# Graph attention, two layers on 32 graphs: keys and values of two tiles by seven half-depth products

## The chip, the core and the metric

The kernel runs on one core of one Trainium2 chip. A core has a matrix engine (TensorE, PE in the profile, with its weight loads as PEld), three engines for elementwise work (VectorE or DVE, ScalarE or ACT, GpSimd or POOL), and a queue engine (SyncE, SP) that issues transfers. Matmuls write to PSUM, eight banks of 2 KB in each of 128 partitions; everything else lives in SBUF. The metric is the time of one execution on the device in microseconds. Five runs of the kernel before gave a median of 2818.61 us (2816.21 to 2819.26).

## The reference

`x` is 32 graphs of 512 nodes with 512 features, `adj` a 512 x 512 matrix of zeros and ones with about 4 ones in a row, one for all graphs. All numbers are float32.

```python
# layer 0
h = relu(layernorm(x))
q, k, v = h @ Wq + bq, h @ Wk + bk, h @ Wv + bv        # 8 heads of 64
scores = q @ k.T / 8 + (1 - adj) * -1e9                # per head
x = x + softmax(scores) @ v @ Wo + bo
# layer 1
h = relu(layernorm(x))
g = h @ W
s1, s2 = g @ a1, g @ a2
e = leaky_relu(s1[:, None] + s2[None, :], 0.2) * adj
x = x + elu(softmax(e) @ g + beta * g)
```

## The kernel before

**Tiles.** A graph is a batch `b` of T = 4 tiles of P = 128 nodes; a tile's features are C = 4 blocks of 128. Since a row of `adj` has few ones, the kernel never forms 512 x 512 scores. It sorts the nodes once (`edges`), so that each group of 32 nodes of a tile has at most 128 edges, and then works on lists of 128 edges: four lists a tile, one for each of the groups `g`. For every batch it

- *stage_a(b)*: fetches x by an indirect transfer (`fetch`, POOL), normalises it (`norm`: DVE, then a power on POOL, line 724, then DVE), applies relu (ACT), turns it by four transposes on TensorE into `hT`, and multiplies `hT` with wk, wv and wq (`dense`, four chained 128x512 products each, recorded at line 41). DVE adds the bias to k and q (line 788), ACT copies v (line 782). SP stores k, v and q to tables in DRAM (`put`).
- *stage_b(b)*: for each tile gathers rows of the table by edge (`kv`, line 826, k and v of layer 0 together with h of layer 1 of the graph two batches earlier) and rows of q (`qe`, line 842), four of each. `layer0` multiplies q by k (line 869), sums by head (line 872), exponentiates and weighs v (ACT, lines 878 and 883: 32 small activations a tile). Then `edge_sums` (line 857) adds up the edges of each node by a product with a 0/1 matrix `OH`: for each group of 32 nodes one product with 32 columns of weights, four groups beside each other in the array. The sums are divided (lines 902, 906), turned, multiplied with wo, added to x (line 920), normalised; the result `hx` is stored for layer 1.
- `layer1` does the same for the graph two batches earlier: weights of edges `wv` (line 994), `edge_sums`, the denominator (lines 1007 to 1009), own share (line 1015), transposes, an addition of column sums (line 1028), the product with W, elu (lines 1037 to 1043), and an indirect store (line 742).

Two row sums at the end of each batch, over v (line 800) and over hx (line 947), use the same array shape as the edge sums, with 512 columns.

**Order.** Nothing is ordered by hand directly. Each step is an `op` with an engine, an estimated duration and a key (its due time, in units where a tile is S = 20). `Plan.order` simulates the engines and takes, of what can start now on an engine, the lowest key; TensorE may wait 0.3 us for a lower key and adds 1.0 to the key of an op of another array shape (`form`). The order so found is the fixed order of every engine's instructions; at run time each waits for what it needs by semaphores. Stage_a of a batch is due six tiles ahead of its stage_b.

**Rings.** Buffers come from `rings`, each with so many buffers; an op that takes one can't be planned before one is free. `reserve` takes the buffer of a result when the product before it starts. PSUM: ring D has 4 banks for all dense products and transposes, ring X has 2 buffers of two banks each for the edge sums. "Free order" rings (D, X) may be taken out of order.

**Batch 0** differs: x comes in plain order, and k, v and q are stored by indirect transfers on POOL, since the sort is not known when it starts.

Of the kernel before, what the change touches and what calls it, by code (L numbers as in the profile page):

```python
# [19 lines left out]
P = 128  # L20
HD = 64
# [191 lines left out]
def kernel(  # L213
# [49 lines left out]
    def ring(n, shape, name):  # L263
# [4 lines left out]
        "hT": ring(2, [P, C, P], "hT"),  # L268
        "oT": ring(2, [P, C, P], "oT"),
        "gT": ring(2, [P, C, P], "gT"),  # L270
        "q": ring(4, [P, D], "q"),
# [3 lines left out]
        "qe": ring(3, [P, 2, D], "qe"),  # L275
        "o": ring(2, [P, D], "o"),
        "x1": ring(4 * LAG + 1, [P, D], "x1"),
        "hx": ring(4, [P, HW_], "hx"),
        "g": ring(2, [P, D], "g"),
        "y": ring(2, [P, D], "y"),  # L280
# [8 lines left out]
        "dn": ring(6, [P, 3], "dn"),  # L289
        "s1": ring(2, [P, T], "s1"),  # L290
        "s1t": ring(1, [T, P], "s1t"),
# [8 lines left out]
        "D": [psum.tile([P, D], F32, name=f"pd{i}", tag=f"pd{i}") for i in range(4)],  # L300
        "X": [psum.tile([P, 2, D], F32, name=f"px{i}", tag=f"px{i}") for i in range(2)],
    }
    plan = Plan(rings, ("D", "X"))
    buf, op = plan.buf, plan.op

    ones = wtile([P, P], "ones")
# [9 lines left out]
    dmax = wtile([P, T, 2], "dmax")  # L316
# [7 lines left out]
        "rmax", "dmax", "bad", "cap", "flag", "perm", "posi",  # L324
    )}

    def setup():
# [3 lines left out]
        nc.gpsimd.memset(ones, 1.0)  # L331
        nc.gpsimd.memset(mhalf, -0.5)
        zero = rings["kv"][-1]
        nc.vector.memset(zero[:, 0, :HW_], 0.0)
# [9 lines left out]
    def constants():  # L344
# [7 lines left out]
        zero = rings["kv"][-1]  # L352
        for tag, n in (("tk", D), ("tkv", D), ("qtab", D), ("th", HW_), ("tab", ROW)):
            for tab in rings[tag]:
                for c0, c1 in ((0, D), (HO, ROW)) if tag == "tab" else ((0, n),):
                    m = 1 if tag == "qtab" else DUMMY
                    load(lambda tab=tab, c0=c0, c1=c1, m=m: nc.sync.dma_start(
                        tab[N:, c0:c1], zero[:m, 0, : c1 - c0]))
# [11 lines left out]
    def edges():  # L370
# [5 lines left out]
        jp, nbb, pr, col = buf("q", "jp"), buf("q", "nb"), buf("q", "pr"), buf("g", "col")  # L376
        sd, val, sc, Eb = buf("kv", "scr2"), buf("kv", "val"), buf("kv", "scr"), buf("kv", "E")

        def flat(b):
            return b.ap.rearrange("p a b -> p (a b)")  # L380
# [42 lines left out]
        op("PE", 1.0, key, lambda: product(nc, pk.ap, ones, flat(sd)[:, :N]), r=[sd], w=[pk])  # L423
# [29 lines left out]
        op("PE", 1.0, key, lambda: product(nc, pp.ap, ones, flat(sd)[:, :N]), r=[sd], w=[pp])  # L453
# [124 lines left out]
        en = buf("kv", "en")  # L578
# [62 lines left out]

    def value_row():
        bvc, bvr = buf("g", "bvc"), buf("oT", "bvr")
# [16 lines left out]
    def dot_rows():  # L660
        wa = buf("s1", "wa"), buf("s1", "wa")
        for g in range(2):
            ar, scr, row = buf("y", "ar"), buf("o", "scr"), buf("row", "wrow")
# [80 lines left out]

    def put(b, dst, t, src, key, part, w):
# [8 lines left out]
    def stage_a(b):  # L754
# [3 lines left out]
        for t in range(T):  # L758
            key = base(T * b + t - AHEAD) if b else 2.0 + 0.4 * S * t
            xb = buf("x", f"x{b}_{t}")  # L760
            if b:
                op("POOL", 1.3, key - 2.0 * S, lambda xb=xb, t=t: fetch(xb.ap, b, t), r=[C_["perm"]], w=[xb], dma=P * D * 4)
            else:
                op("SP", 0.1, -90.0 + 0.01 * t, lambda xb=xb, t=t: nc.sync.dma_start(xb.ap, x[0, ts(t, P), :]), w=[xb], dma=P * D * 4)
            norm(key - 1.3 * S, xb, mv, t, f"a{b}_{t}")
            op("ACT", 0.8, key - 0.9 * S, lambda xb=xb, t=t: relu(xb.ap, xb.ap, mv.ap, t), r=[(mv, t)], w=[xb])
            pt, hT = buf("D", "pt"), buf("hT", f"hT{b}_{t}")
            o = op("PE", 0.45, key - 0.51 * S, lambda pt=pt, xb=xb: turned(pt.ap, xb.ap), r=[xb], w=[pt])
            plan.reserve(o, hT)

            op("ACT", 0.6, key - 0.51 * S, lambda pt=pt, hT=hT: nc.scalar.copy(  # L771
                hT.ap.rearrange("p c q -> p (c q)"), pt.ap), r=[pt], w=[hT])
            q, k, v = buf("q", f"q{b}_{t}"), buf("k", f"k{b}_{t}"), buf("v", f"v{b}_{t}")
            vs.append(v)
            for i, (w, n, dst) in enumerate(((wk, "wk", k), (wv, "wv", v), (wq, "wq", q))):
                p = buf("D", "p" + n)
                kk = key + (0.12, 0.30, 0.56)[i] * S
                o = op("PE", 3.43, kk, lambda p=p, hT=hT, w=w: dense(p.ap, hT.ap, w),
                       r=[hT, C_[n]], w=[p])
                plan.reserve(o, dst)  # L780
                if n == "wv":
                    op("ACT", 0.62, kk, lambda p=p, v=v: nc.scalar.copy(  # L782
                        v.ap[:, :, 0:HD], p.ap.rearrange("p (h f) -> p h f", f=HD)), r=[p], w=[v])
                    tab, cols = place(b, VO, H * VW)
                    put(b, cols, t, lambda v=v: v.ap.rearrange("p h f -> p (h f)"), kk, v, [(tab, ("v", t))])
                else:
                    row = {"wq": bq_r, "wk": bk_r}[n]
                    op("DVE", 0.7, kk, lambda p=p, dst=dst, row=row: nc.vector.tensor_tensor(  # L788
# [27 lines left out]
    def stage_b(b):  # L816
# [14 lines left out]
        for t in range(T):  # L831
# [16 lines left out]
            if old is not None:  # L848
                layer1(b - LAG, t, kb, slots)
# [445 lines left out]
```

## Time and profile before

| | |
|---|---|
| median of five runs | 2818.61 us |
| profiled execution, its own time | 2821.35 us |
| its span, first to last instruction | 2819.6 us |
| mean granted TensorE clock | 0.991 |
| dense products (line 41: wo, wk, w, wv, wq), records | 1032 + 4 x 1024 |
| edge sums (line 857), records | 2 x 2048 |
| transposes (line 712), records | 640 + 512 + 512 |
| DMA, mean rate | 283 GB/s, 796.83 MB |
| windows 300 to 800, 800 to 1300, 1300 to 1800 us | TensorE busy 500.00 of 500 in each; DMA share 0.84, 0.84, 0.86 |
| last 119 us | TensorE busy 91.5, DMA share 0.59 |

A float32 product is two records of matmul, so a dense product of four blocks is eight records; the durations given for single matmuls overlap, and times between starts are what counts. Rows of groups give line, engine, operation, output and inputs by the program's names, shape and count; then busy time and the mean of one in ns; then the idle time of the engine just before them and what ended it. A row of the waits gives engine, what was about to run, what it waited for, the time in all, how often, and the longest.

### The profile page before, as it was taken

How to read it: one execution, taken by the hardware profiler on the slowest of the kernel's cores; microseconds unless marked ns; L12 is line 12 of the kernel's file. 1: busy time of each engine (PE TensorE's matmuls, PEld its weight loads, DVE VectorE, ACT ScalarE, POOL GpSimd, SP SyncE). 2: the span in 40 equal slices, each digit the busy share in tenths (PEclk: the TensorE clock that was granted, in tenths of full speed). 3: DMA queues.
4: the chain of work that ended last, by engine and by line, in shares of the span. 5: the costliest groups of instructions: out<-in, count | busy, mean ns of one | idle time of the engine just before them, and what ended most of it. 6: DMA issues, size and time to landing. Idle time of an engine off the chain costs nothing. (4 is left out here: it accounts for less than half of the span.)

```text
span 2819.6 us, 41845 instructions
## 1 busy us (share of the span) xinstructions
PE 2759.1 (98%) x11506; PEld 1290.9 (46%) x11506; DVE 1894.5 (67%) x4556; ACT 1940.5 (69%) x6241; POOL 1890.0 (67%) x1730
## 2 busy tenths in 40 slices
PE   7999999999999999999999999999999999999977
PEld 3444444444444444444444444444444444444433
DVE  6466667666666666666666666666766666666674
ACT  1476777676677677677677677677677777677774
POOL 2787666676666676666676766666766666666665
PEclk9999999999999999999999999999999999999989
DMA  5889888888888888888888888888888888888875
GB/s 166 233 292 328 301 297 288 287 291 284 299 295 287 287 289 289 298 293 293 284 287 293 293 292 298 279 288 297 290 291 300 276 287 302 284 294 295 274 252 149
DMA packets 242344, 796.83 MB, mean 283 GB/s; under 512 B 35587, under 2 KB 35715, under 8 KB 242102
## 3 DMA queue, kind: packets, MB, share of 16 engines
q0 software_dynamic: 157056, 643.94, 68.1%
q1 hardware_dynamic: 85046, 150.15, 14.8%
q8 instruction: 93, 1.52, 0.2%
q14 instruction: 149, 1.22, 0.1%
HBM read 624.70 MB, written 169.26 MB: 282 GB/s over the span
## 5 line engine op out<-in xcount | busy, mean ns | idle before, releaser
L883 ACT ACTIVATE kv<-kv 128x64 f32<-128x64 f32 x4096 | 1006.2, 335 | 6.2
L826 POOL DMA_INDIRECT kv<-tab,idx x480 | 517.3, 1078 | 331.8 <-PE px L857 219.0
L842 POOL DMA_INDIRECT qe<-qtab,qidx x512 | 555.1, 1084 | 177.5 <-issue 123.4
L869 DVE TENSOR_TENSOR qe<-qe,kv 128x1024 f32<-128x1024 f32 x256 | 313.6, 1225 | 282.1 <-DMA kv<-tab,idx 171.0
L41 PE MATMUL pd<-wo,oT 128*128 128x512 f32 x1032 | 475.2, 604 | 8.9 <-DVE k L788 4.5
L41 PE MATMUL pd<-wk,hT 128*128 128x512 f32 x1024 | 474.0, 606 | 0.3 <-ACT hT L771 0.3
L41 PE MATMUL pd<-w,gT 128*128 128x512 f32 x1024 | 463.1, 595 | 2.6 <-ACT gT L1028 2.6
L41 PE MATMUL pd<-wv,hT 128*128 128x512 f32 x1024 | 462.8, 595 | 0.7 <-ACT hT L771 0.7
L41 PE MATMUL pd<-wq,hT 128*128 128x512 f32 x1024 | 460.9, 593 | 0.8 <-ACT v L782 0.8
L737 POOL DMA_INDIRECT x<-in_x_dram,perm x252 | 340.8, 1352 | 78.5 <-issue 49.6
L724 POOL TENSOR_TENSOR mv<-mv,mhalf 128x1 f32<-128x1 f32 x256 | 225.0, 881 | 202.1 <-DVE mv L721 161.7
L872 DVE TENSOR_REDUCE s<-qe 128x16 f32<-128x1024 f32 x256 | 310.7, 1214 | 2.1
L41 PEld LDWEIGHTS pd<-wo,oT 128*128 128x128 f32 x1032 | 196.9, 194 | 247.7 <-issue 232.8
L41 PEld LDWEIGHTS pd<-wv,hT 128*128 128x128 f32 x1024 | 195.4, 191 | 246.2 <-issue 238.5
L41 PEld LDWEIGHTS pd<-w,gT 128*128 128x128 f32 x1024 | 194.3, 191 | 247.2 <-issue 237.1
L41 PEld LDWEIGHTS pd<-wk,hT 128*128 128x128 f32 x1024 | 185.6, 190 | 250.5 <-issue 204.9
L41 PEld LDWEIGHTS pd<-wq,hT 128*128 128x128 f32 x1024 | 187.3, 190 | 201.2 <-issue 199.5
L782 ACT COPY v<-pd 128x512 f32<-128x512 f32 x128 | 74.5, 582 | 264.2 <-PE pd L41 264.2
L731 ACT ACTIVATE x<-x,mv 128x512 f32<-128x512 f32 x128 | 104.1, 813 | 188.0 <-DVE mv L726 135.9
L920 DVE TENSOR_TENSOR x<-pd,x 128x512 f32<-128x512 f32 x128 | 88.4, 691 | 181.5 <-PE pd L41 171.6
L742 POOL DMA_INDIRECT out_dram<-y,perm x128 | 156.6, 1223 | 60.1 <-issue 18.5
L719 DVE BATCH_NORM_STATS2 st<-x 128x6 f32<-128x512 f32 x256 | 176.2, 688 | 14.8 <-DMA x<-in_x_dram 6.7
(180 smaller groups left out, 3166.7 us busy)
## 6 DMA issues: line engine op xcount, KB each, us to landing
qtab<-q SPq DMA_DIRECT2D x124, 256.0 KB
tab<-hx SPq DMA_DIRECT2D x120, 260.0 KB
tab<-v SPq DMA_DIRECT2D x120, 260.0 KB
tab<-k SPq DMA_DIRECT2D x120, 256.0 KB
qe<-qtab,qidx POOLq DMA_INDIRECT x512, 6.6
q<-row SPq DMA_DIRECT2D x32, 256.0 KB
kv<-tab,idx POOLq DMA_INDIRECT x480, 7.1
x<-in_x_dram,perm POOLq DMA_INDIRECT x252, 7.7
```

The lines of the kernel that those rows point to most:

```text
L41: nc.tensor.matmul(out, lhsT, rhs, start=start, stop=stop)
L719: nc.vector.bn_stats(s6.ap, src.ap)
L724: op("POOL", 0.75, key, lambda: nc.gpsimd.tensor_tensor(mv.ap[:, t, 2:3], mv.ap[:, t, 2:3], mhalf[:, 0:1], op=ALU.pow), w=[(mv, t)])
L731: nc.scalar.activation(dst, src, AF.Relu, bias=mv[:, t, 3:4], scale=mv[:, t, 2:3])
L737: nc.gpsimd.indirect_dma_start(dst, None, rows, bass.IndirectOffsetOnAxis(ap=perm[:, t : t + 1], axis=0), **lim)
L742: nc.gpsimd.indirect_dma_start(rows, bass.IndirectOffsetOnAxis(ap=perm[:, t : t + 1], axis=0), src, None, **lim)
L826: nc.gpsimd.indirect_dma_start(dst, None, tab.ap, bass.IndirectOffsetOnAxis(ap=idx[:, t, g : g + 1], axis=0), bounds_check=N + DUMMY - 1, ...
L842: op("POOL", 1.3, kb - 0.84 * S + 0.1 * g, lambda q=qs[g // 2], g=g, t=t: nc.gpsimd.indirect_dma_start(q.ap[:, g % 2, :], None, s["qtab"]. ...
L869: nc.vector.tensor_tensor(qe.ap, qe.ap, sl.ap[:, :, KO : KO + D], op=ALU.mult)
L872: nc.vector.tensor_reduce(sb.ap, qe.ap.rearrange("p n (h f) -> p n h f", f=HD), axis=AX.X, op=ALU.add)
L883: nc.scalar.activation(p[:, h, 0:HD], p[:, h, 0:HD], AF.Copy, scale=p[:, h, HD : HD + 1])
L920: op("DVE", 0.7, k + 0.9 * S, lambda: nc.vector.tensor_tensor(x1.ap, pw.ap, x1.ap, op=ALU.add), r=[pw], w=[x1])
```

## The change

The rows of k and v of two tiles are one product of matrices: [h0; h1], split at half of the features into A11, A12 (tile 0) and A21, A22 (tile 1), times [wk | wv], split at half of its rows into B11, B21 (wk) and B12, B22 (wv). Done plainly this takes eight half-depth products, each two chained 128x512 products. The new code takes seven, by Strassen's scheme in the form with four sums on the left and four on the right. The four sums of weights are made once (`right_sums`): T1 = B12 - B11 replaces the upper half of wv once batch 0 has used it, and wt2, wt3, wt4 are new. The four sums of features S1 to S4 are made on DVE for each pair of tiles. One PSUM buffer, p1, starts with A11 B11, has S2 wt2, then S3 wt3, then A22 wt4 added to it, and is read in between; p5 holds S1 T1, then S4 B22 on top. Batch 0 keeps the plain products (`plain_keys_and_values`).

The edge sums are cut otherwise: 512 columns of features into one bank, and the sums of weights (8 columns in layer 0, 2 in layer 1) into a slot of a shared bank `small`. Ring X has so two single banks, D five. Other rings shrink or are merged: o, g and y share `w`. `dn` is one buffer for a batch, and `dmax` is updated once a batch, not once a tile. `ones` lives in a buffer of x1 and the zero row in one of qe. Three estimated durations of the planner change.

```diff
     rings = {
-        "hT": ring(2, [P, C, P], "hT"),
-        "oT": ring(2, [P, C, P], "oT"),
-        "gT": ring(2, [P, C, P], "gT"),
-        "q": ring(4, [P, D], "q"),
+        "hT": ring(3, [P, C, P], "hT"),
+        "S": ring(3, [P, C // 2, P], "S"),
+        "oT": ring(1, [P, C, P], "oT"),
+        "gT": ring(1, [P, C, P], "gT"),
+        "q": ring(2, [P, D], "q"),
...
-        "qe": ring(3, [P, 2, D], "qe"),
-        "o": ring(2, [P, D], "o"),
+        "qe": ring(2, [P, 2, D], "qe"),
+        "w": ring(4, [P, D], "w"),
...
-        "g": ring(2, [P, D], "g"),
-        "y": ring(2, [P, D], "y"),
...
-        "dn": ring(6, [P, 3], "dn"),
+        "dn": ring(3, [P, 3, T], "dn"),
...
-        "D": [psum.tile([P, D], F32, name=f"pd{i}", tag=f"pd{i}") for i in range(4)],
-        "X": [psum.tile([P, 2, D], F32, name=f"px{i}", tag=f"px{i}") for i in range(2)],
+        "D": [psum.tile([P, D], F32, name=f"pd{i}", tag=f"pd{i}") for i in range(5)],
+        "X": [psum.tile([P, D], F32, name=f"px{i}", tag=f"px{i}") for i in range(2)],
     }
+    small = psum.tile([P, 4, 16], F32, name="small", tag="small")
+    rings["small"] = [small[:, i, :] for i in range(4)]
...
+    K2 = C // 2
+    B11, B21, B22, T1 = wk[:, :K2, :], wk[:, K2:, :], wv[:, K2:, :], wv[:, :K2, :]
+    TK = 36.0
+    def right_sums():
+        def sub(name, dst, a, b, r, w):
+            for c in range(K2):
+                op("DVE", 0.7, TK + 0.01 * c, lambda c=c: nc.vector.tensor_tensor(
+                    dst[:, c, :], a[:, c, :], b[:, c, :], op=ALU.subtract), r=r(c), w=[(C_[name], c), *w(c)])
+        none = lambda c: []
+        sub("t3", wt3, B22, T1, lambda c: [(C_["wv"], c), (C_["wv"], K2 + c)], none)
+        sub("t1", T1, T1, B11, lambda c: [(C_["wk"], c)], lambda c: [(C_["wv"], c)])
+        sub("t2", wt2, B22, T1, lambda c: [(C_["t1"], c), (C_["wv"], K2 + c)], none)
+        sub("t4", wt4, B21, wt2, lambda c: [(C_["t2"], c), (C_["wk"], K2 + c)], none)
...
+    def turned_state(b, t, key, mv):
...
+        kt = key + ((0.48, -0.51)[t % 2] if b else -0.51) * S
+        o = op("PE", 0.45, kt, lambda: turned(pt.ap, xb.ap), r=[xb], w=[pt])
...
+    def keys_and_values(b, t, key, h0, h1):
+        k = [buf("k", f"k{b}_{t + i}") for i in range(2)]
+        v = [buf("v", f"v{b}_{t + i}") for i in range(2)]
+        A11, A12, A21, A22 = (lambda h=h, c=c: h.ap[:, c : c + K2, :] for h in (h0, h1) for c in (0, K2))
+        S1, S2, S3, S4 = (buf("S", f"S{i}") for i in range(1, 5))
+        ks = key - 0.3 * S
+        def left_sum(dst, a, b, how, r):
+            op("DVE", 0.36, ks, lambda: nc.vector.tensor_tensor(dst.ap, a(), b(), op=how), r=r, w=[dst])
+        left_sum(S1, A21, A22, ALU.add, [h1])
+        left_sum(S2, lambda: S1.ap, A11, ALU.subtract, [S1, h0])
+        left_sum(S3, A11, A21, ALU.subtract, [h0, h1])
+        left_sum(S4, A12, lambda: S2.ap, ALU.subtract, [S2, h0])
+        p1, p2, p5 = buf("D", "pu"), buf("D", "pp2"), buf("D", "pp5")
+        def half(kk, p, lhs, rhs, r, first=True, take=None):
+            def prod():
+                for c in range(K2):
+                    nc.tensor.matmul(p.ap, lhs()[:, c, :], rhs[:, c, :], start=first and c == 0, stop=c == K2 - 1,
+                                     skip_group_check=True)
+            o = op("PE", 1.72, key + kk * S, prod, r=r, w=[p])
+            if take is not None:
+                plan.reserve(o, take)
+        def add(kk, dst, a, b, r):
+            op("DVE", 0.7, key + kk * S, lambda: nc.vector.tensor_tensor(dst(), a(), b(), op=ALU.add), r=r[:-1], w=[r[-1]])
...
+        half(0.10, p1, A11, B11, [h0, (C_["wk"], 0), (C_["wk"], 1)], take=k[0])
+        add(0.10, lambda: k[0].ap, lambda: p1.ap, lambda: bk_r, [p1, C_["rows"], k[0]])
+        half(0.16, p2, A12, B21, [h0, (C_["wk"], 2), (C_["wk"], 3)])
+        add(0.16, lambda: k[0].ap, lambda: p2.ap, lambda: k[0].ap, [p2, k[0]])
+        store_k(b, t + 0, k[0], key + 0.16 * S)
+        half(0.22, p1, lambda: S2.ap, wt2, [S2, C_["t2"]], False, take=v[0])
+        op("ACT", 0.62, key + 0.22 * S, lambda: nc.scalar.copy(vals(0), heads(p1)), r=[p1], w=[v[0]])
+        half(0.34, p1, lambda: S3.ap, wt3, [S3, C_["t3"]], False, take=v[1])
+        op("ACT", 0.62, key + 0.34 * S, lambda: nc.scalar.copy(vals(1), heads(p1)), r=[p1], w=[v[1]])
+        half(0.62, p5, lambda: S1.ap, T1, [S1, C_["t1"]])
+        add(0.62, lambda: vals(1), lambda: heads(p5), lambda: vals(1), [p5, v[1]])
+        store_v(b, t + 1, v[1], key + 0.62 * S)
+        half(0.68, p1, A22, wt4, [h1, C_["t4"]], False, take=k[1])
+        add(0.68, lambda: k[1].ap, lambda: p1.ap, lambda: bk_r, [p1, C_["rows"], k[1]])
+        store_k(b, t + 1, k[1], key + 0.68 * S)
+        half(0.74, p5, lambda: S4.ap, B22, [S4, (C_["wv"], 2), (C_["wv"], 3)], False)
+        add(0.74, lambda: vals(0), lambda: heads(p5), lambda: vals(0), [p5, v[0]])
+        store_v(b, t + 0, v[0], key + 0.74 * S)
+        return v
...
-        for t in range(T):
-            key = base(T * b + t - AHEAD) if b else 2.0 + 0.4 * S * t
...
-            for i, (w, n, dst) in enumerate(((wk, "wk", k), (wv, "wv", v), (wq, "wq", q))):
-                kk = key + (0.12, 0.30, 0.56)[i] * S
...
+        for t in range(0, T, 2):
+            keys = [base(T * b + u - AHEAD) if b else 2.0 + 0.4 * S * u for u in (t, t + 1)]
+            hT = [turned_state(b, u, key, mv) for u, key in zip((t, t + 1), keys)]
+            vs += keys_and_values(b, t, keys[1], *hT) if b else plain_keys_and_values(t, keys, hT)
+            for u in range(2):
+                queries(b, t + u, keys[1] + (0.28, 0.9)[u] * S if b else keys[u] + 0.56 * S, hT[u])
...
-    def edge_sums(px, lhs, slots, c0, cuts):
-        for h, (c1, n) in enumerate(cuts):
+    def edge_sums(parts, lhs, slots):
+        for out, cols in parts:
             for g in range(NG):
                 nc.tensor.matmul(
-                    px[ts(g, G), h, 0:n], lhs(g), slots[g // 2].ap[:, g % 2, c0 + c1 : c0 + c1 + n],
-                    start=True, stop=True,
+                    out(g), lhs(g), cols(slots[g // 2].ap[:, g % 2, :]), start=True, stop=True,
                 )
...
-            op("DVE", 1.37, key, mult, r=[sl], w=[qe])
+            op("DVE", 1.24, key, mult, r=[sl], w=[qe])
...
+        parts = (
+            (lambda g: px.ap[ts(g, G), :].rearrange("p (h f) -> p h f", f=HD), lambda row: val(row)[:, :, 0:HD]),
+            (lambda g: pa.ap[ts(g, G), 0:H], lambda row: val(row)[:, :, HD]),
+        )
...
-        op("DVE", 0.94, k + 1.1 * S, lambda: dot(hx.ap[:, D : D + 1], wa2_r), r=[(C_["wa"], 1)], w=[hx, scr])
+        op("DVE", 0.78, k + 1.1 * S, lambda: dot(hx.ap[:, D : D + 1], wa2_r), r=[(C_["wa"], 1)], w=[hx, scr])
...
+        parts = (
+            (lambda g: px.ap[ts(g, G), :], lambda row: row[:, HO : HO + D]),
+            (lambda g: pa.ap[ts(g, G), 0:2], lambda row: row[:, HO + D : HO + D + 2]),
+        )
...
-        op("DVE", 0.4, k + 0.6 * S, lambda: nc.vector.tensor_tensor(
-            dmax[:, t, :], dmax[:, t, :], dn.ap[:, 0:2], op=ALU.max), r=[dn], w=[(C_["dmax"], t)])
```

## The prediction

> **What bounds the kernel now.** I first read the page: busy times, then the windows.
>
> ```profile
> span 2819.6 us, 41845 instructions
> PE 2759.1 (98%) x11506; PEld 1290.9 (46%) x11506; DVE 1894.5 (67%) x4556; ACT 1940.5 (69%) x6241; POOL 1890.0 (67%) x1730
> ```
>
> TensorE is busy for 98% of the span. That alone proves little, since ends of matmuls are modelled, so I looked at a stretch of two tiles in the middle (the table of windows: length, then busy time of PE, PEld, DVE, ACT, POOL, granted clock, DMA share, GB/s) and at TensorE's timeline inside it.
>
> ```profile
> 1402.30:1443.40 41.10, 41.10 (x165) 19.27 (x168) 28.36 (x61) 27.18 (x92) 28.86 (x26) 1.00 0.87 306
> ```
>
> ```profile
> 1403.65 3.70 PE L41 MATMUL pd<-wk,hT 128*128 128x512 f32 x8
> 1407.19 3.60 PE L41 MATMUL pd<-wv,hT 128*128 128x512 f32 x8
> 1410.62 0.60 PE L712 MATMUL pd<-ident,o 128*128 128x128 f32 x4
> 1411.06 0.60 PE L712 MATMUL pd<-ident,g 128*128 128x128 f32 x4
> 1411.50 0.60 PE L712 MATMUL pd<-ident,x 128*128 128x128 f32 x4
> 1411.93 3.60 PE L41 MATMUL pd<-wq,hT 128*128 128x512 f32 x8
> 1415.37 3.60 PE L41 MATMUL pd<-wo,oT 128*128 128x512 f32 x8
> 1418.80 3.60 PE L41 MATMUL pd<-w,gT 128*128 128x512 f32 x8
> 1422.33 1.07 PE L857 MATMUL px<-kv,wv 128*32 128x256 f32 x16
> 1423.22 1.06 PE L857 MATMUL px<-kv,OH 128*32 128x260 f32 x16
> ```
>
> The reader is to see that every line begins where the one before ends, with no idle time in brackets, at full clock. A tile's period is the sum of its matmuls: the layer-0 edge sums at 1423.22 had started at 1402.64 for the tile before, 20.58 us earlier. In the trace TensorE has no gap over 0.02 us between 253 and 2665 us. So whatever leaves TensorE's list leaves the time, as long as the others keep up. DVE is busy 28.36 of 41.10 us, ACT 27.18, and the DMA engines 0.87 of it: the nearest second bound is the DMA.
>
> **The products.** A dense product of a tile is eight records and lasts start to start 3.43 us (1415.37 to 1418.80). Batch 0 stays plain; batches 1 to 31 have two pairs of tiles each, 62 pairs. Keys and values of a pair were four dense products, that is eight half-depth ones of 1.717 us; now they are seven. Saved: 62 x 1.717 = 106.4 us.
>
> **The edge sums.** There are 256 (128 per layer). Before, two cuts of about 260 columns: 0.89 us from the first (1422.33) to the next group of the same array shape (1423.22). Now one part of 512 columns and one of 8 (layer 0) or 2 (layer 1). The trace has the large part already, in the two sums over rows that end a batch:
>
> ```profile
> 448.05 1.04 PE L800 MATMUL pd<-v,one 128*32 128x512 f32 x8
> 448.91 1.04 PE L947 MATMUL pd<-hx,one 128*32 128x512 f32 x8
> 449.88 1.55 PE L41 MATMUL pd<-wk,hT 128*128 128x512 f32 x3
> ```
>
> 0.86 us from 448.05 to 448.91; the first reads its values in strides as the new line will, so the stride costs nothing. The small part has no row. From below it is 0 (hidden in the entry of the next group). From above: the nearest small products are those with 18 columns in the set-up (line 41, 128x18, 32 records in 3.6 us), 0.112 us each. In the px groups the four column tiles of a pass start 6 to 7 ns apart, so eight records make two passes, 0.22 us. Without that overlap it would be 8 x 0.112 = 0.9, which the px rows exclude (16 records in 0.89). I take 0.10, between these but nearer to the px form with its short weights: 0.86 + 0.10 - 0.89 = +0.07, x 256 = +18 us, with ends of -0.03 (-8 us) and +0.19 (+49 us).
>
> The Trainium skill ("TensorE: Matmul & The Clock Gate", section "Wait — 56ns, not 53.3ns?") speaks against small matmuls: start to start never falls below about 25 ns however few the columns. By it alone eight records would take 0.20 us and the change would cost 0.17 x 256 = 44 us (an estimate from that page) instead of 18. The trace has starts of 6 to 7 ns across column tiles, so the floor, if it binds, binds per column tile.
>
> **DVE.** Per pair there are four left sums of 128x256 and three more adds of 128x512 (five where there were two):
>
> ```profile
> L788 DVE TENSOR_TENSOR k<-pd,bk_r 128x512 f32<-128x512 f32 x128 | 88.4, 691 | 62.7 <-PE pd L41 62.4
> L612 DVE TENSOR_TENSOR kv<-kv,kv 128x256 f32<-128x256 f32 x1 | 0.4, 424 | 0.0
> ```
>
> 4 x 0.424 + 3 x 0.691 = 3.77 us a pair; the dmax update goes from four to one a batch (0.148 each), 0.22 us a pair back. DVE's busy time rises from 28.36 to 31.9 per pair, beside a TensorE that needs some 39.5: 81%. It is not the bound, and on throughput costs nothing. Its cover is 7 us a pair. ACT's list is unchanged, two copies for v.
>
> **The new waits.** Now p1 is one PSUM bank that is written, read, and added to again: S2's product waits for the DVE add of k0, S3's for ACT's copy of v0, A22's for ACT's copy of v1; S4's waits on p5 for DVE. Between p1 and S2 in key order stands p2, 1.72 us, against an add of 0.69: 1.0 us of margin, which semaphore and queue must fit into. Between S2 and S3 stands a full query product (3.43), against a copy of 0.6. A late answer stops TensorE, and behind it everything. What makes DVE late are waits in its queue:
>
> ```profile
> DVE qe L869 <- DMA kv<-tab,idx: 171.0, 69, 4.7
> DVE qe L869 <- issue: 104.3, 41, 3.5
> PE px L857 <- ACT kv L883: 6.0, 6, 2.1
> ```
>
> 110 of 256 score products keep DVE waiting, 2.5 us on average (171.0/69 and 104.3/41), with k and q additions queued behind. Before, four rotating banks hid this. A wait that falls on such a place costs 2.5 - 1.0 = 1.5 us. Bounds: 0 (the planner puts the add ahead), and two such waits in each pair, 3.0 x 62 = 186 us. I take one wait in every fifth pair, 0.3 us: +19 us. That is nearer to the lower end, because the planner's margins have left the middle without a single gap.
>
> **Banks and rings, one by one.** D grows from 4 to 5 while p1 holds one for most of a pair: about as many free as before, 0. "small" is four slots in one bank; a DVE read of the weights' sum (line 1007) may now have to wait until the next edge sums end, about 1.0 us later on DVE. Line 1007 began at 1423.47, its result feeds the transposes of g one tile's third later (1411.06 in the tile shown, some 7 us after its edge sums): hidden; if uncovered, 1 us x 128. The Trainium skill ("PSUM — Partial Sum Buffer", section "PSUM bank collisions raise a hardware error") asks that two engines be kept apart by bank and quadrant, not by address, so slots in one bank are ordered as one. No row of before shows two slots in one bank. By the rule the 1 us is certain, by the rows it is covered.
>
> qe goes from 3 to 2. POOL's gathers of queries then wait until the DVE reduction of the same half of the tile before. In the trace a reduction ended at 1430.72, the two query gathers ran to 1436.66, they take 6.6 us to land, and the product that follows them ran at 1442.42: nothing to spare for that wait, but ACT finished weighing a tile 22 us before its edge sums (1421.67 for those at 1443.78), so a few us on DVE are covered. What queues behind on POOL are the x fetch, the store of y and the pow of line 724. kv stays at 5; the loop edge sums, gather, score, weigh takes about 18 of 41 us. oT and gT with one buffer are free 10 us before the next transposes. w: o, g, y and the scratch row live some 8, 8, 18 and 5 us in 20: two of four slots. All 0; if the cover goes, each is a TensorE wait as above. Set-up: eight DVE subtractions, 5.5 us, needed only by batch 1; zero fills from another ring, same bytes. SP issues k, v and q stores as before, one each per tile, of the same bytes, but those of the first tile of a pair later, and in the order k0, v1, k1, v0; a store that waits for a late add holds the hx stores behind it. The gathers that need either are over a tile away: 0; without that cover POOL, and all gathers behind, would wait as long as the add is late. +1 us for the start. In the last 119 us TensorE is already partly idle; its edge sums are counted above.
>
> **Sum**, against the profiled execution's own 2821.4 us (span 2819.6): -106.4 + 18 + 19 + 1 = -68.4, giving 2753. The median of the runs is 2.7 us below that execution: 2750. Bounds of the terms alone: 2818.6 - 106.4 - 8 = 2704 to 2818.6 - 106.4 + 49 + 186 + 1 = 2948.
>
> **Rivals.**
> (1) Nothing waits and the small part is nearly hidden: 2818.6 - 106.4 + 0 to 13 = 2712 to 2725. For it: no gap in the middle before. Against: four tight hand-backs a pair. 0.17.
> (2) The DMA becomes the bound. A batch of four tiles has a period of 84.8 us, share 0.86: 72.9 us of DMA. The gain would shrink it to 82, a share of 0.89. If the rest can't work above 0.87, the highest window of the middle, the batch is 83.8, 1.0 us shorter, x 31 = 31: 2788. For it: DVE's waits are on gathers, and qe loses a buffer. Against: between 140 and 300 us the share was 0.90 at 310 GB/s. 0.18, 2785 to 2812.
> (3) Slower: p1's hand-backs, by the mechanism above. Place: between p1 and S2 and between p5 and S4, both answered by DVE. Two uncovered waits cost 3.0 us a pair; the pair's gain is 1.717 - 4 x 0.07 = 1.44. It decides from 48% of the pairs on. At two thirds of the pairs: 2818.6 - 106.4 + 18 + 124 = 2854. For it: 110 of 256 products wait, and DVE gets 13% more work. Against: the order is by readiness, so an add that is ready need not stand behind a gather. 0.19.
> (4) No change, all terms cancelling: 0.04.
>
> **Chances.** The forecast, 2725 to 2785, has 0.42. A difference under 0.2%, 5.6 us, is about what this kernel's runs can't tell from none. Faster: 0.42 + 0.17 + 0.18 = 0.77; same 0.04; slower 0.19. The range, 2712 to 2832, leaves out about 0.06 below and 0.14 above, the worst of rival 3.
>
> **What would show it.** Right: seven groups of four records on wk, wv and the new weights per pair, each 1.72 us; px groups of 128x512 and 128x8 with under 0.2 us more per group; TensorE idle under 40 us more in the waits; batch period near 82.3 us. Wrong: TensorE waiting on k or v additions (DVE) or v copies (ACT) for over 90 us in all; a DMA share above 0.88 with TensorE waiting for ACT's weighing; small parts above 0.3 us; a lower clock from new gaps.

## The result, and the profile after

Before takes 2819.49 us and after 2824.61 us, medians of 49 and 29 runs; the ratio is 1.0017, 95% interval 1.0012 to 1.0022. The forecast was 2750 us. So the change makes the kernel slower by 0.17%, 5 us: less than the 5.6 us that the prediction held for hard to tell from none, but with this many runs clear of none. The profiled execution took 2821.48 us, span 2819.6, by chance the span of before.

The page of after, first lines:

```profile
span 2819.6 us, 41737 instructions
PE 2697.3 (96%) x11258; PEld 1216.7 (43%) x11258; DVE 2073.9 (74%) x4902; ACT 1939.7 (69%) x6241; POOL 1876.6 (67%) x1730
```

TensorE has 248 matmuls fewer, as 62 pairs of 4 should give, is 61.8 us less busy, and the span has not moved. So the work went and idle time came in its place. To size it without the modelled ends, I counted for every matmul its columns at 0.429 us per 512, the spacing of dense records in the trace, a quarter of that for the column-tiled ones (edge sums and row sums), and called the sum the stream. The rest of the span is lost time, here cut at 400 us of stream from the start and 300 us from the end:

| | stream us | lost us | start | middle | end |
|---|---|---|---|---|---|
| before | 2662.1 | 157.4 | 50.4 | 42.6 | 64.4 |
| after | 2555.7 | 263.9 | 73.3 | 101.9 | 88.7 |
| difference | -106.4 | +106.5 | +22.9 | +59.3 | +24.3 |

The stream is a count and no measurement: 248 records fewer at 0.429 us are 106.4. What is measured is that a half-depth product takes 1.72 us in its place (below, 1421.36 to 1423.08), so the saving is real, and that the span stays: all of it is given back as lost time.

A stretch of two tiles of after (windows: length, then busy time of PE, PEld, DVE, ACT, POOL, granted clock, DMA share, GB/s):

```profile
1376.00:1417.90 41.90, 41.07 (x169) 18.24 (x165) 34.93 (x79) 35.37 (x118) 30.57 (x28) 1.00 0.86 297
```

The clock is full and the DMA share no higher than before, 0.86: the transfers are not what has become late. Over 470 to 2400 us the same view has PE at 1930.00 of 1930 us before and 1897.59 after, the clock 1.00 and the DMA share 0.85 in both. Outside that stretch the clock is lower: 0.94 in after between 200 and 290 us, where before has 1.00, and over the whole span 0.986 against 0.991. That is the sign of "a lower clock from new gaps" which the prediction named; in the start it can cost some 5 us (0.06 of 90 us, an estimate).

TensorE's timeline of after, the same kind of place as shown of before (start, length, then the matmuls; in brackets the idle time before them and what ended it). In the kernel after, line 959 is the edge sums, line 837 a half-depth product, line 731 the transposes:

```profile
1378.22 1.76 PE L731 MATMUL pd<-ident,w 128*128 128x128 f32 x12 [0.55 <-DVE w L1120]
...
1392.33 1.04 PE L959 MATMUL px<-kv,OH 128*32 128x512 f32 x8
...
1393.35 1.98 PE L837 MATMUL pd<-wt,S 128*128 128x512 f32 x4
1395.17 3.60 PE L41 MATMUL pd<-wq,hT 128*128 128x512 f32 x8
1398.60 1.88 PE L837 MATMUL pd<-wt,S 128*128 128x512 f32 x4
1400.32 1.04 PE L731 MATMUL pd<-ident,w 128*128 128x128 f32 x8
...
1413.21 3.60 PE L41 MATMUL pd<-wq,hT 128*128 128x512 f32 x8
1416.74 1.06 PE L959 MATMUL px<-kv,wv 128*32 128x512 f32 x8
1417.62 0.22 PE L959 MATMUL small<-kv,wv 128*32 128x2 f32 x8
1417.68 1.04 PE L959 MATMUL px<-kv,OH 128*32 128x512 f32 x8
1418.54 0.22 PE L959 MATMUL small<-kv,OH 128*32 128x8 f32 x8
1418.69 1.53 PE L731 MATMUL pd<-ident,x 128*128 128x128 f32 x12
1420.27 1.26 PE L731 MATMUL pd<-ident,w 128*128 128x128 f32 x8
1421.36 1.88 PE L837 MATMUL pd<-wk,hT 128*128 128x512 f32 x4
1423.08 3.60 PE L41 MATMUL pd<-w,gT 128*128 128x512 f32 x8
...
1430.04 1.06 PE L959 MATMUL px<-kv,wv 128*32 128x512 f32 x8
```

Two things are to be seen. The small parts cost next to nothing: 1417.62 to 1417.68 is 0.06 us, and from one group of edge sums to the next, 1416.74 to 1417.68, it is 0.94 us, against 0.89 before. And in every second tile the transposes of o and g (`ident,w`) now stand right behind the edge sums that they are made from (1418.54, then 1420.27). Before, the prediction's fence had wk and wv between, 7 us of work in which DVE divided. In the middle of before the median from the start of the last record of the edge sums to these transposes is 7.28 us; in after it alternates from tile to tile, 7.1 to 8.9 us and 1.7 to 3.0 us. The seven products of a pair and both its query products carry keys of the odd tile. At that time the edge sums of tiles 0 and 2 of a batch are due, and products stand behind those (1393.35 to 1400.32); behind the edge sums of tiles 1 and 3 there is little to do but the transposes of x.

The waits of after, TensorE's and then DVE's (what was to run, what it waited for, time in all, how often, the longest):

```profile
PE pd L731 <- DVE w L1120: 41.4, 50, 2.3
PE pd L731 <- ACT x L750: 18.9, 8, 6.5
PE pd L731 <- DVE w L1007: 13.4, 10, 4.2
...
PE pd L837 <- DVE v L845: 3.5, 1, 3.5
PE pd L837 <- ACT v L861: 3.2, 6, 0.9
```

```profile
DVE dn L1112 <- PE small L959: 125.1, 96, 5.5
```

The like rows of before:

```profile
PE pd L712 <- DVE g L1015: 4.6, 3, 3.3
PE pd L712 <- DVE o L906: 4.0, 3, 2.2
```

```profile
DVE dn L1007 <- PE px L857: 49.6, 84, 4.7
```

What ends most of TensorE's waits now is DVE's own share (line 1120) and division (line 1007), ahead of the transposes, not the hand-backs of p1 and p5 (the last two lines of the first block). The row of `dn` says why line 1120 is late: `dn`, which it needs, waited 125.1 us for `small`, where before it waited 49.6 us for its sums. The row of line 750, the relu of x, lies wholly outside 470 to 2400 us.

### The profile page after: what moved, and what is told of

It reads as the page before. It is cut to its first block, busy times and chain, and to the rows that moved or that the text cites. A ratio compares the mean times of both kernels' runs of the same rounds, so it can differ in the third digit from the quotient of the medians.

```text
span 2819.6 us, 41737 instructions
## 1 busy us (share of the span) xinstructions
PE 2697.3 (96%) x11258; PEld 1216.7 (43%) x11258; DVE 2073.9 (74%) x4902; ACT 1939.7 (69%) x6241; POOL 1876.6 (67%) x1730
## 4 chain that ended last, share of the span: by engine, by line
PE 74%; DVE 7%; issue 4%; ACT 2%; DMA 2%; POOL 2%; POOLq 0%; DVEq 0%; ACTq 0%
PE pd L41 40%; PE pd L837 22%; PE px L959 7%; PE pd L731 4%; ACT kv L984 1%; DVE w L1120 1%; DVE s L973 1%; DMA qe<-qtab,qidx 1%; DMA x<-in_x_dram,perm 1%; DVE w L1007 1%; PE small L959 1%; POOL kv L925 1%; DVE qe L970 0%; DVE w L1144 0%; DVE w L1143 0%
## 5 line engine op out<-in xcount | busy, mean ns | idle before, releaser
L756 POOL DMA_INDIRECT x<-in_x_dram,perm x252 | 363.0, 1441 | 84.2 <-issue 57.1
L970 DVE TENSOR_TENSOR qe<-qe,kv 128x1024 f32<-128x1024 f32 x256 | 312.6, 1221 | 77.2 <-issue 41.8
L743 POOL TENSOR_TENSOR mv<-mv,mhalf 128x1 f32<-128x1 f32 x256 | 183.5, 718 | 233.1 <-DVE mv L740 185.7
L837 PE MATMUL pd<-wk,hT 128*128 128x512 f32 x496 | 242.0, 612 | 7.5 <-DVE cs L1055 5.7
L761 POOL DMA_INDIRECT out_dram<-w,perm x128 | 150.5, 1176 | 136.3 <-DVE z L1094 68.8
L837 PE MATMUL pd<-wv,S 128*128 128x512 f32 x496 | 235.2, 597 | 3.5 <-DVE v L845 3.5
L837 PE MATMUL pd<-wt,S 128*128 128x512 f32 x496 | 236.0, 598 | 0.0
L1138 ACT ACTIVATE w<-pd,dn 128x512 f32<-128x512 f32 x128 | 87.1, 681 | 204.1 <-PE pd L41 203.8
L731 PE MATMUL pd<-ident,w 128*128 128x128 f32 x1152 | 164.7, 281 | 59.1 <-DVE w L1120 41.4
L979 ACT ACTIVATE kv<-s 128x16 f32<-128x16 f32 x256 | 59.5, 233 | 186.9 <-DVE s L973 181.8
L731 PEld LDWEIGHTS pd<-ident,w 128*128 128x128 f32 x1152 | 128.9, 142 | 121.2 <-DVE w L1120 55.4
```

Of the source, the lines that this page charges most:

```text
L731: nc.tensor.transpose(p[:, ts(c, P)], src[:, ts(c, P)], ident)
L743: op("POOL", 0.75, key, lambda: nc.gpsimd.tensor_tensor(mv.ap[:, t, 2:3], mv.ap[:, t, 2:3], mhalf[:, 0:1], op=ALU.pow), w=[(mv, t)])
L756: nc.gpsimd.indirect_dma_start(dst, None, rows, bass.IndirectOffsetOnAxis(ap=perm[:, t : t + 1], axis=0), **lim)
L761: nc.gpsimd.indirect_dma_start(rows, bass.IndirectOffsetOnAxis(ap=perm[:, t : t + 1], axis=0), src, None, **lim)
L837: nc.tensor.matmul(p.ap, lhs()[:, c, :], rhs[:, c, :], start=first and c == 0, stop=c == K2 - 1, skip_group_check=True)
L970: nc.vector.tensor_tensor(qe.ap, qe.ap, sl.ap[:, :, KO : KO + D], op=ALU.mult)
```

## The experiments

Four theories. **A**: the merged ring `w` is handed out strictly in order of key, so the planner can't start the next tile's edge sums (which reserve o and g) until W's product of the tile before has reserved its y; with the products of a pair gone to one of the two tiles, nothing is left to stand between edge sums and transposes in the other. **B**: the slots of `small` are one bank and are ordered as one, so `dn` of layer 1 waits until layer 0's edge sums behind it have ended too, 0.94 us later. **C**: the planner's durations for DVE and ACT are too long. **D**: the forecast's rival, hand-backs of p1 and p5. Ratios are to the kernel before on the same chip; the groups ran on different chips, and absolute times aren't compared between them. The runs of the result and the first group, where before takes 2819.49 and 2818.05 us, are called the first chip below, whether it was one or two alike.

**First group** (before 2818.05 us there).

w_free: ring w out of order.

```diff
-    plan = Plan(rings, ("D", "X"))
+    plan = Plan(rings, ("D", "X", "w"))
```

> The changed kernel with one edit: the merged ring w may hand out its buffers in any order, like D and X. Theory A (the order that the ring enforces: the edge sums of the next tile reserve their buffer of w and so can't stand ahead of the W product of the tile before, which leaves nothing between edge sums and the transposes that wait for them): the waits of TensorE before the transposes mostly go, the time falls by 25 to 50 us, to 2775 to 2800. Theory B (the bank that the small sums share, which delays DVE by a group of edge sums): the waits before the transposes stay, under 10 us of change. Theory D (hand-backs of p1 and p5, the forecast's rival): no change.

2786.54 us, ratio 0.989 (0.9874 to 0.9907); lost time 228.6 = 77.3 + 77.5 + 73.8. One word in the planner gives 24.4 us of the middle and 14.9 of the end, and takes 4.0 at the start. Its timeline shows how:

```profile
1410.17 1.06 PE L959 MATMUL px<-kv,wv 128*32 128x512 f32 x8
...
1411.12 1.04 PE L959 MATMUL px<-kv,OH 128*32 128x512 f32 x8
1411.98 0.22 PE L959 MATMUL small<-kv,OH 128*32 128x8 f32 x8
1412.13 1.09 PE L731 MATMUL pd<-ident,x 128*128 128x128 f32 x8
1413.71 0.66 PE L731 MATMUL pd<-ident,w 128*128 128x128 f32 x4 [0.48 <-DVE w L1120]
1414.29 1.07 PE L959 MATMUL px<-kv,wv 128*32 128x512 f32 x8
```

The next tile's edge sums start 4.1 us after the first ones (1410.17 to 1414.29), in among the transposes; in after they came 13.3 us later (1416.74 to 1430.04). Over the whole span the wait for line 1120 halves:

```profile
PE pd L731 <- DVE w L1120: 21.0, 22, 3.7
```

before_w: the counter-test, the old kernel with o, g and y merged into one ring of the same six buffers, in order of key.

```diff
-        "o": ring(2, [P, D], "o"),
-        "g": ring(2, [P, D], "g"),
-        "y": ring(2, [P, D], "y"),
+        "w": ring(6, [P, D], "w"),
```

> The kernel before with only its rings o, g and y merged into one ring w of six buffers, taken in key order; no other part of the change. Theory A: gaps before transposes appear that the kernel before has not, and it gets slower by 20 to 60 us (2840 to 2880). Theories B and D: six buffers are as many as before, nothing changes (within 5 us of 2819).

2841.14 us, 1.0083 (1.0066 to 1.01). The order alone costs 23 us in a kernel that has no Strassen and not a buffer less. But most of it comes at the end, where 81.3 us are lost instead of 64.4; the middle loses 52.2 instead of 42.6, and the start 43.3, 7 less. TensorE's wait for DVE's own share, 4.6 us in before, grows:

```profile
PE pd L710 <- DVE w L1013: 20.4, 13, 3.5
```

yet none of it lies between 470 and 2400 us: wk and wv still stand behind the edge sums there, 7.28 us in the median, and TensorE's only wait is 7.4 us, of transposes for a copy on ACT. So A is shown by w_free, and the counter-test shows that this order costs time in itself. That the middle pays more for it where the products behind the edge sums are gone (24.4 us by w_free, 9.6 here) fits A, but no run shows it alone.

den_px: `dn` reads a column of the 512-column sums in place of its sum of weights, so layer 1's result is not the reference's; no read of layer 1 waits for `small` any more.

```diff
-            nc.vector.tensor_scalar_add(dn.ap[:, 0, t : t + 1], pa.ap[:, 1:2], float(N))
+            nc.vector.tensor_scalar_add(dn.ap[:, 0, t : t + 1], px.ap[:, 1:2], float(N))
```

> The changed kernel, same order of all instructions; the first of the three DVE operations of the denominator reads a column of the edge sums' own bank (px) in place of the small bank, so that it waits only for its own group. This leaves the right denominator of layer 1 out. Theory B: the 125 us that DVE waits there shrink to about 50, transposes start some 0.9 us earlier per tile where they wait, and 20 to 50 us of the time go (2775 to 2805). Theory A: TensorE still has nothing to do there; at most half of its 60 us of waits go, 5 to 25 us (2800 to 2820).

2794.23 us, 0.9916 (0.9898 to 0.9934); middle 74.1 us lost instead of 101.9. From the start of layer 1's edge sums to `dn` it is 1.1 us in most tiles before, 2.1 after, 1.2 to 1.3 here. Between 470 and 2400 us TensorE's wait for line 1120 is 19.7 us in after, and here:

```profile
PE pd L731 <- DVE w L1120: 0.9, 1, 0.9
```

B is shown as far as an edit goes that also changes what is read; small_first and free_banks below keep the result.

estimates: durations of DVE and ACT in the planner times 0.9 and 0.92.

```diff
+        us = us * {"DVE": 0.9, "ACT": 0.92}.get(eng, 1.0)
```

> The changed kernel with the planner's durations for DVE times 0.9 and for ACT times 0.92, nearer to what the trace shows start to start. Theory C (the order is made for engines slower than they are): a tighter order, 20 to 45 us less (2780 to 2805). Theory A: the ring's order stays, under 15 us.

2821.61 us, 1.0011 (1.0002 to 1.0021): C falls. The middle loses some 89 us, less than after, but the start 82 and the end 92, more.

**Second group** (another chip, before 2854.77 us). small_first exchanges the two parts of layer 0's edge sums, 8 columns first, so that `dn` of layer 1 is released 0.06 us and not 0.94 us after its own group; free_first is this with w free; free_first_est scales the durations as well, by 0.92 and 0.94.

```diff
-            (lambda g: px.ap[ts(g, G), :].rearrange("p (h f) -> p h f", f=HD), lambda row: val(row)[:, :, 0:HD]),
             (lambda g: pa.ap[ts(g, G), 0:H], lambda row: val(row)[:, :, HD]),
+            (lambda g: px.ap[ts(g, G), :].rearrange("p (h f) -> p h f", f=HD), lambda row: val(row)[:, :, 0:HD]),
```

> The changed kernel with the two parts of layer 0's edge sums exchanged: the 8 small columns first, then the 512. The small sums of both layers then follow each other, and DVE waits for one short pass more instead of a whole group. Same order of everything else, full result. Theory B (the shared bank) as the run with the wrong denominator had it: 25 to 30 us off the changed kernel, 2792 to 2802. If that run was faster because it left a read out: under 8 us off, above 2815.

> The changed kernel with both edits: w in any order, and layer 0's small columns first. If A and B shorten and fill the same gap (edge sums to transposes), the effects overlap: 2770 to 2784. If they are separate losses they add, 38 + 28: about 2758. If one hides the other: 2784 to 2788, as with w alone.

> Both edits and the planner's durations for DVE times 0.92, for ACT times 0.94. Theory C in a weak form (once the ring doesn't hold the order, truer durations pay): 5 to 20 us below the run with both edits. If the durations don't matter: within 4 us of it.

1.0042 (1.0025 to 1.0059), 0.9943 (0.9927 to 0.996) and 1.0043 (1.0027 to 1.006). The first two lie far above what the first group let expect, and w free gave 1.0%, where it was 1.3% in the first group: either the exchange does nothing, or this chip shows the kernel after otherwise. The kernel after was not in the group, so it was inconclusive. Scaled durations cost 1.0% here: C falls again.

rest_alone leaves out the scheme: plain keys and values in all batches, no `right_sums`; rings, banks and cuts stay as after.

```diff
-            vs += keys_and_values(b, t, keys[1], *hT) if b else plain_keys_and_values(t, keys, hT)
+            vs += plain_keys_and_values(b, t, keys, hT)
```

> The changed kernel without the scheme: keys and values of all batches by plain products as in batch 0, no sums of weights; new edge sums, banks and rings stay. Theory A and B: the rest of the change by itself costs what the scheme saves: the merged ring 23 us, the bank and the edge sums 15 to 40 us, so 2850 to 2880. Theory D (the loss is in the scheme's own hand-backs and in DVE's extra work): the rest costs little, 2815 to 2835.

1.0096 (1.0079 to 1.0113): what was done to make room costs about 1% by itself, a little less than the 1.011 to 1.022 of before that A and B had let expect. The transposes still start 7.08 us behind the last record of the edge sums, in the median. Its lost time is 215 us, 71 of them in the middle; the profiles of before and after on two other chips where before takes some 2850 us (fifth and third group) have 187 and 338, 50 and 163 of them in the middle. As far as these chips compare, most of the loss comes only with the ring, the bank and the split products together.

**Third group** (before 2851.86 us): the kernel after as the level, and the open pairs. w_free_den has w free and the read of den_px.

> The kernel after, unchanged, as the level for the other three of this chip. A and B both: 1.0017 of the kernel before (1.000 to 1.004); if the chip changes the ratio, it is about 1.006 to 1.010, as the four kernels of the slower chip would suggest.

> Layer 0's two parts exchanged, the 8 columns first; nothing else. B (DVE waits because the bank of the small sums is counted as one, so a 512-column group of 0.9 us stands between it and its number): 15 to 30 us less than the kernel after on this chip (0.989 to 0.995 of it), as the read of px gave 0.9916 of the kernel before. If the wait is the bank's and DVE had other work, or the exchange makes layer 0's own reader wait instead: within 0.3% of the kernel after, or slower.

> Both single edits together: w taken as ready and not in order of key, and the denominators read a column of the 512-column sums (so the result of layer 1 is not the reference's). If A and B are two separate losses, their gains add up: 1.0017 - 0.0127 - 0.0101 = 0.979 of the kernel before (0.976 to 0.983). If both relieve one and the same place, the transposes behind the edge sums, the second adds little: 0.985 to 0.990.

> w taken as ready, and layer 0's 8 columns first. A alone: as w_free on the other chip, 0.989 of the kernel before (0.986 to 0.992). A and B adding: 0.978 to 0.984. If the chip changes the ratio: 0.994, as on the slower chip.

The kernel after is at 1.0183 (1.0159 to 1.0208) here, small_first at 1.0046 (1.0031 to 1.0061), free_first at 0.9977 (0.9961 to 0.9992), w_free_den at 0.9902 (0.9877 to 0.9926). The chip was the answer: against the kernel after beside it, 2902.06 us, the exchange of two lines gives 1.3% (2864.43) and keeps the result, which is B; TensorE's wait for line 1120 falls from 66.0 to 31.2 us. With w free as well it gives 2.0% (2844.55), and w free with the read of den_px 2.8% (2821.84). Singly, in the first group, w free and that read gave 1.3 and 1.0%. They are two losses, not one, though w free adds only 0.7% to the exchange here. Against before, both pairs missed what adding up had let expect (0.976 to 0.983 and 0.978 to 0.984), since the kernel after itself stands 1.7% higher here than on the first chip.

**Fourth group** (before 2838.74 us). free_banks: w free, and the small sums of the two layers in a bank each, the second taken from ring D. free_late: w free, and the seven products only from batch 2 on.

```diff
-        "D": [psum.tile([P, D], F32, name=f"pd{i}", tag=f"pd{i}") for i in range(5)],
+        "D": [psum.tile([P, D], F32, name=f"pd{i}", tag=f"pd{i}") for i in range(4)],
...
-        px, pa, g = buf("X", f"pg{b}_{t}"), buf("small", "pa"), buf("w", f"g{b}_{t}")
+        px, pa, g = buf("X", f"pg{b}_{t}"), buf("small1", "pa"), buf("w", f"g{b}_{t}")
```

> The kernel after, unchanged, as the level for the other three of this chip: 1.0017 of the kernel before if the chip is like the first one, 1.018 if it is like the one of the run before this.

> w taken as ready, and layer 1's denominators read from the 512-column sums (so the result of layer 1 is not the reference's). On a chip where the kernel after is at 1.0017 of before: if A and B are two separate losses, 0.979 (0.976 to 0.983), some 2760 us where before takes 2819, near the forecast's 2750; if they relieve one and the same place, 0.985 to 0.990. On a chip where after is at 1.018: 0.990 again.

> w taken as ready, and the small sums of the two layers in a bank each (D has four banks for it instead of five). B (the wait is for the one bank): most of den_px's gain without touching the result, 0.978 to 0.985 where after is at 1.0017. If the fifth bank of D is what the products with their additions need, TensorE waits for DVE's and ACT's hand-backs instead: 0.990 or more.

> w taken as ready, and the seven products only from batch 2 on (60 pairs, so 3.4 us more work for TensorE); the eight subtractions then wait for batch 1. If the scheme's first batch costs the start its 20 to 27 us (time without a matmul streaming in the first 400 us of the stream is 79.5 with w free, 52.6 in the kernel before), that falls to 50 to 60 and the whole to 0.981 to 0.984 where w free alone gives 0.989. If the start is slow for another cause (smaller rings in the set-up), it stays at 75 or more and the whole at 0.989 to 0.992.

after 1.0168 (1.0151 to 1.0185), w_free_den 0.988 (0.986 to 0.99), free_banks 0.9933 (0.991 to 0.9956), free_late 1.0013 (1.0003 to 1.0022). Lost time in the middle: 148.8 in after, 84.8 in w_free_den, 97.3 in free_banks. So free_banks is 2.5% faster than the kernel after (2813.62 against 2886.87 us) with the reference's result. Four banks for D do cost something: its largest wait of TensorE in the middle is now a hand-back, 13.6 us for `DVE k`, where w_free_den beside it has 5.7.

free_late was a miss: the start loses 86.2 us, no less than 79.9 in after and 86.9 in w_free_den beside it. The sums over hx of batches 0, 1 and 2 stand 74.6 and 112.7 us apart, in w_free on the first chip 83.7 and 98.2, in after 90.5 and 83.0, in before 73.4 and 84.8. So the loss seems to move on with the first paired batch, but the spacing of one run doesn't show it. In rest_alone, with the small rings and without the scheme, the start loses 53.2: so it goes with the scheme rather than with the set-up's smaller rings. Between 130 and 470 us TensorE's largest named wait is that of the transposes of x for relu: 7.8 us in after, 5.5 in w_free, 10.2 in free_late; before and rest_alone have no such row there. That is about a third of the start's 23 us; why relu is late, and the rest, stay open.

**Fifth group** (before 2851.48 us). The kernel before for its profile, and free_banks with layer 0's small part first.

> The kernel before, unchanged, for its profile on a chip like the last two, where before takes 2839 to 2855 us: if the chip makes TensorE's signals reach DVE later, the four small-bank reads of a batch that start 1.1 us after their edge sums on the first chip start 2 to 5 us after them here, and the time without a matmul streaming in the middle rises from 53 to some 75 to 85 us. If only other things are slower (transfers, gathers), these reads stay at 1.1 us.

> w taken as ready, the two layers' small sums in a bank each, and layer 0's 8 columns first. If DVE's wait for layer 0's small sums still matters: 0.3 to 0.6% under free_banks (0.987 to 0.990 of the kernel before where after is at 1.017). If the banks apart have already taken it: 0.993 again.

before_again shows reads of `dn` 2.4 to 6.1 us, mostly 4.6 or more, after the start of their edge sums in every fourth tile, where the first chip had 2.4 to 3.6, but nearly all others stay at 1.1 us, and the middle loses 50.4 us, not 75: of the two expectations neither. The start loses 65.1 and the end 71.2, against 50.4 and 64.4. free_banks_first is at 0.9914 (0.9896 to 0.9932) to free_banks' 0.9933 on another chip: no difference that these intervals can tell.

## Why the prediction was wrong

2824.61 us lies inside the stated range, 2712 to 2832, but that is luck: the range is wide, and the waits that came are not those that it was made of. No rival, and no sign of being wrong, named the ring or the bank.

**The products**: right, 106.4 us of stream less, at 1.72 us a half-depth product. **The edge sums**: right in kind, and under the forecast: 0.05 us a group, about 13 us for 256 where 18 were taken. **DVE, and the DMA as a rival**: right that neither is the bound. The batch period in the middle is 83.9 us (before 84.8), close to that rival's 83.8, but for another reason: with w free it is 82.9 at a DMA share of 0.87, so the transfers could go faster all along.

**The rings failed.** "w: o, g, y and the scratch row live some 8, 8, 18 and 5 us in 20: two of four slots. All 0;" I counted slots and not the rule by which a ring is handed out, though the list of rings that may be taken out of order stood in the text. Three rings in order of key each are no constraint between o, g and y; one ring in order of key is. It was put at 0; price: 1.3% on the first chip (w_free), 0.8% even in the kernel before.

**The shared bank failed.** The delay was foreseen and nearly at its size, "about 1.0 us later on DVE", measured 1.0 us (`dn` 2.1 instead of 1.1 us behind the start of its edge sums); it was costed at nothing, "hidden", by the 7 us between edge sums and transposes. That cover was real before, 7.28 us, but it consisted of the very products that the change takes apart and gathers behind the edge sums of every second tile; behind the others 1.7 to 3.0 us are left. So the forecast priced an edit by the old order. Price: 1.0% on the first chip (28 us, not the 128 us named for no cover at all), 1.3% on the third.

**The hand-backs were a term of the wrong size and place.** The 19 us for p1 are 3.2 us of waits for ACT's copy on the first chip, and 5.1 for DVE's additions, so the slower rival fell there. On the third chip a part of it comes back, still far from the 90 us that were to show it: TensorE's wait in after_again is

```profile
PE pd L837 <- ACT v L861: 22.5, 13, 2.0
```

**Start and end failed**: +1 us and nothing were written, +22.9 and +24.3 us came. The end goes with w for 14.9 of its 24.3 us (73.8 lost with w free; 81.3 in before_w against 64.4), the start with the scheme, cause open.

**The whole**: the two edits together take 80 and 81 us off the kernel after on the third and fourth chip (2902.06 to 2821.84, 2886.87 to 2805.78). On the first their singles add up to 0.0228 of before, some 64 us, an estimate; both together were not run there. Of the 59.3 us more that its middle loses, w_free took back 24.4 and den_px 27.8; if these add, 7 are left, about what the small parts cost there (0.05 us for some 184 groups, 9 us, an estimate). No kernel that ran came down to the forecast's 0.976 of before: the start's 23 us and a part of the end are still lost. The saving of the scheme was sized rightly; that it would meet no new wait but the hand-backs was the mistake.

Versions that keep the result and beat both kernels: w_free on the first chip (2786.54 us, where before takes 2818.05), free_banks on the fourth (0.9933 of before, 0.975 of after).

## What to carry to other kernels

An edit that is hidden is hidden by named work: when the same change moves or splits that work, price the edit without it. When rings are merged, ask not only how many buffers are alive at once, but in what order they are given out and which step that order now ties to which. A saving on the bound engine is kept only if the released order still has filler behind each producer that another engine must answer; count the filler between such pairs, before and after.

## What the runs showed of the hardware

Chips differ, and more for one kernel than for the other. TensorE runs the same list at the same spacing, 0.429 us from record to record of a dense product, and the span of after is 2819.6 us on the first chip and 2894.1 on the third; before has 2819.6 on the first and 2848.8 on the fifth, where its median is that of the third. The kernel after loses two and a half times as much. Durations of instructions are alike (weighing on ACT 336 and 335 ns, the product on DVE 1221 and 1221 ns in after), and the gathers' queue held the transfer engines 1.3% longer in after (30859 and 31272 us, summed over 16). After the transposes of a batch's sums the next ones start 0.83 us later on the first chip, and 2.8 to 3.1 us later on the third in every second batch. What is late there I can't say: the profiles of these chips lack a good quarter of the semaphore records (29887 against 42089), and the releasers that they name are less sure for it.

A part of it is the clock. In the middle (470 to 2400 us) the granted clock of after_again drops to half in eleven stretches of 3.4 or 6.8 us, 41 us in all, ten of them at a place where two starts of matmuls stand 2.5 to 3.1 us apart; dense records start 0.853 us apart there. After has one such stretch on the first chip, 3.4 us, and before_again none. So up to 20 of the 61 us that the middle loses more on the third chip lie in these stretches (an estimate, half of 41).

A column-tiled group of eight records with 2 or 8 columns takes 0.06 us start to start, 7 to 8 ns a record.
